# Attention scores in two column halves of TensorE, two query tiles in a row

## The chip, the core and the metric

The kernel runs on one core of one Trainium2 chip. The metric is device time in microseconds (us) from the start to the end of one execution, taken as the median of the runs. A core has five engines that run side by side, each through its own list of instructions in order: TensorE (PE) multiplies matrices, with PEld its loading of the stationary operand; VectorE (DVE) and ScalarE (ACT) work on rows of 128 partitions[...]; GpSimd (POOL)[...]; SyncE (SP) issues DMAs. They meet through semaphores.

## The reference

Two transformer layers with adaptive layer norm, in fp32, on x of 4 x 512 x 512. The first layer is small. The second holds nearly all of the time: attention with 32 query heads of 128 in 8 groups (four query heads share one key and one value head), causal, over 512 positions, for 4 batches; then a gated feed-forward layer of width 1792.

```python
q = (hidden_states @ w_q).reshape(B, S, Hkv, g, D)
k = (hidden_states @ w_k).reshape(B, S, Hkv, D)
v = (hidden_states @ w_v).reshape(B, S, Hkv, D)
scores = jnp.einsum('bqhgd,bkhd->bhgqk', q, k) * scale
causal = jnp.tril(jnp.ones((S, S), dtype=bool))
scores = jnp.where(causal, scores, -jnp.inf)
probs = jax.nn.softmax(scores.astype(jnp.float32), axis=-1).astype(q.dtype)
attn = jnp.einsum('bhgqk,bkhd->bqhgd', probs, v)
attn = attn.reshape(B, S, Hq * D)
return attn @ w_o
```

The change concerns the line of `scores`, the causal mask, and what follows them up to the softmax.

## The kernel before

The first 209 us compute the first layer and the first projections. From 209 to about 1709 us runs the attention of the second layer, and after it the feed-forward layer.

**Blocks, heads, tiles.** There are 32 blocks n (4 batches x 8 key heads), each with four query heads, so 128 heads s in all, and 64 pairs of heads. A head's 512 queries are four tiles i of 128. Because of the causal mask, tile i needs the keys up to (i + 1) x 128 only. `score(s, i)` (L872 to L887) makes one product on TensorE, 128 queries by (i + 1) x 128 keys, into a PSUM bank (L878); VectorE adds the mask to the last 128 columns (L879) and takes the negated maximum of each row (L881); ScalarE writes the exponentials to SBUF with their sums (L883). `divide` (L889) takes the reciprocal of the sum on VectorE and multiplies on ScalarE; `flip` (L895) transposes blocks of 32 x 32 on VectorE. When a pair is done, `carry` (L911) issues 16 DMAs that complete the transposition, and `value` (L920) multiplies the transposed probabilities with the values and copies the result from PSUM to `oT` on ScalarE (L933).

**Projections.** q, k, v and the output projection are done by Strassen's scheme with seven products. A product is a piece: `seven` (L738) writes it to a bank called `quarter` (L746), and VectorE adds it to what it belongs to (L778, L780, L842); the first of each seven is copied by ScalarE (L786).

**Order.** The order of work on each engine is that in which the program issues it. `window(w, ...)` (L1120) is the unit: it scores pair w + 1 and multiplies pair w with its values. Its eight score tiles go into slots 0 to 7: first head's tiles 3, 2, 1, 0, then the second head's. In slot i the program issues the transposition of the tile two slots back, the division of the tile one slot back, the score of this slot's tile, and then this slot's share of the projection pieces and of side work (statistics of a layer norm, or reads of weight blocks for their largest magnitude, L954). The two value products come in slots 8 and 9. Windows of two kinds alternate: one carries the pieces of q and part of k or v, the other the pieces of the output projection and the rest of k or v.

**Banks.** [...] Scores rotate through four: pools `ps_mm` and `ps_tr`, two banks each, taken in turn by the parity of i (L875), so that a tile's product waits for the exponentials of the tile four slots earlier. The pieces and half of the value products share three banks (`ps_sc`), and one bank is for the other value products.

Of the kernel before, what the change touches and what calls it, by code (L numbers as in the profile page):

```python
# [8 lines left out]
F32 = mybir.dt.float32  # L9
# [4 lines left out]
ALU = mybir.AluOpType  # L14
# [3 lines left out]
P = 128  # L18
# [6 lines left out]
HKV, G, D1 = 8, 4, 128  # L25
INTER = 1792
FB = 256
EPS = 1e-5
NEG = -3.0e38
EXACT = 4096.0  # L30


@with_exitstack
def adaln_two_layers(ctx: ExitStack, tc: tile.TileContext, a, out: bass.AP):
    nc = tc.nc
# [9 lines left out]
    conste = early.enter_context(tc.tile_pool(name="conste", bufs=1))  # L45
    lnp = early.enter_context(tc.tile_pool(name="ln", bufs=1))
    gap = early.enter_context(tc.tile_pool(name="gate_a", bufs=B))
    ps_mm = early.enter_context(tc.tile_pool(name="ps_mm", bufs=2, space=PSUM))
    ps_sc = early.enter_context(tc.tile_pool(name="ps_sc", bufs=3, space=PSUM))
    ps_tr = early.enter_context(tc.tile_pool(name="ps_tr", bufs=2, space=PSUM))  # L50
# [83 lines left out]
    with tc.using_default_side("right"):  # L134
# [15 lines left out]
    nc.vector.memset(mhalf, -0.5)  # L150
    ident = const.tile([P, P], F32, name="ident")
    make_identity(nc, ident)
    mask = conste.tile([P, P], F32, name="mask")
    nc.gpsimd.memset(mask, 0.0)
    nc.gpsimd.affine_select(
        out=mask, in_=mask, compare_op=ALU.is_ge, fill=NEG, base=0,
        pattern=[[-1, P]], channel_multiplier=1,
    )

    o_sb = [l0w.tile([P, NT, 32], F32, name=f"o{b}") for b in range(B)]  # L160
    for b in range(B):
# [3 lines left out]
        cid, pattern=[[0, 1]], base=0, channel_multiplier=1,  # L165
# [54 lines left out]
    ADD, SUB = ALU.add, ALU.subtract  # L220
# [5 lines left out]
    def left_sums(eng, t, s):  # L226

        A11, A21, A12, A22 = quarters(t)
        S3, S2, S4 = s[:, 0], s[:, 1], s[:, 2]
        eng.tensor_tensor(S3, A11, A21, SUB)  # L230
        eng.tensor_tensor(A21, A21, A22, ADD)
        eng.tensor_tensor(S2, A21, A11, SUB)
        eng.tensor_tensor(S4, A12, S2, SUB)
        return {1: A11, 2: A12, 3: S4, 4: A22, 5: A21, 6: S2, 7: S3}
# [15 lines left out]
    def sums_in(kind, n):  # L250
        w = weights[kind, n]
        s = T["wp"].tile([P, 3, 2, w.shape[2] // 2], F32, tag=f"s{kind}", name=f"s{kind}")
        left[kind, n] = left_sums(nc.gpsimd, w, s)
# [455 lines left out]
    for o in order:  # L709
        name, _, eng = o.partition("/")  # L710
# [24 lines left out]
    def bank(shape, name):  # L735
        return ps_sc.tile(shape, F32, tag="sc", name=name)
# [18 lines left out]
    qT, kT, vs, oT, prob = {}, {}, {}, {}, {}  # L755
# [8 lines left out]
    def sums_h(b, engs):  # L764
        s = hp.tile([P, 4, 2, HALF], F32, tag="hT", name="hsum")
        right["h", b] = right_sums(engs, h1[b], [s[:, i] for i in range(3)], s[:, 3])
# [40 lines left out]
    def q_pieces(n):  # L807
        def start():
            for j in range(2):
                qT[n, j] = at.tile([P, 2, S], F32, tag="qT", name="qT", bufs=3)  # L810
            return corners(qT[n, 0], qT[n, 1])

        return seven(lambda: left["q", n], lambda: right["h", n // HKV], gather(start), SEVENTH)
# [37 lines left out]
    BK = 32  # L851
    NG = P // BK
# [13 lines left out]
    def blocks(s, i):  # L866

        if s // 2 == LAST:
            return plain[:, s % 2, i, : (i + 1) * P].rearrange("p (j q) -> p j q", q=BK)
        return prob2[s // 2 % 2][:, : NG * (i + 1), s % 2, i, :]  # L870

    def score(s, i):  # L872
        n, h = divmod(s, G)
        w = (i + 1) * P
        pool, tag = ((ps_mm, "mm"), (ps_tr, "tr"))[i % 2]  # L875
        ps = pool.tile([P, 512], F32, tag=tag, name="sc")
        q = qT[n, h // 2][:, h % 2, :]
        nc.tensor.matmul(ps[:, :w], q[:, i * P : w], kT[n][:, :w], start=True, stop=True)  # L878
        nc.vector.tensor_tensor(ps[:, i * P : w], ps[:, i * P : w], mask, ADD)  # L879
        nmx = small.tile([P, 1], F32, tag="nmx", name="nmx")  # L880
        nc.vector.tensor_reduce(nmx, ps[:, :w], AX.X, ALU.max, negate=True)  # L881
        den = small.tile([P, 1], F32, tag="den", name="den")
        nc.scalar.activation(  # L883
            blocks(s, i), ps[:, :w].rearrange("p (j q) -> p j q", q=BK),
            AF.Exp, bias=nmx, accum_out=den,
        )
        prob[s, i] = den  # L887

    def divide(s, i):  # L889
        p = blocks(s, i)  # L890
        rden = small.tile([P, 1], F32, tag="rden", name="rden")
        nc.vector.reciprocal(rden, prob.pop((s, i)))  # L892
        nc.scalar.mul(p, p, rden)  # L893
# [17 lines left out]
    def carry(pair):  # L911

        for a_ in range(NG):
            src = prob2[pair % 2][a_ * BK : (a_ + 1) * BK]
            src = src.rearrange("r (k j) h i q -> r j k (h i q)", j=NG)
            for j in range(NG):
                dst = turned[j * BK : (j + 1) * BK, :, a_]
                nc.sync.dma_start(dst, src[:, j])

    def value(s):  # L920

        n, h = divmod(s, G)
        if h == 0:
            oT[n] = at.tile([P, G, S], F32, tag="oT", name="oT")
        av = bank([P, 512], "av") if s % 2 else ps_av.tile([P, 512], F32, tag="av", name="av")
        pT = straight if s // 2 == LAST else turned
        for k in range(NT):
            nc.tensor.matmul(  # L928
                av.rearrange("p (a n) -> p a n", a=NG)[:, :, BK * k :], vs[n][:, k, :],
                pT[:, k, :, P * (s % 2) + BK * k : P * (s % 2 + 1)],  # L930
                start=(k == 0), stop=(k == NT - 1),
            )
        nc.scalar.copy(  # L933
            oT[n][:, h, :].rearrange("p (i a q) -> p a i q", a=NG, q=BK),
            av.rearrange("p (a i q) -> p a i q", a=NG, q=BK),
        )


    def scan(i):
# [122 lines left out]
    def decide():  # L1062
        size = small.tile([P, 1], F32, tag="size", name="size", bufs=1)
        nc.vector.tensor_reduce(size, sizes, AX.X, ALU.max)
        nc.vector.tensor_scalar(size, size, EXACT, None, ALU.is_gt)
        return size
# [9 lines left out]
    def split_pieces(got):  # L1076

        def piece(c):
            if c == 0:
                h2[0] = [hp.tile([P, KC, S], F32R, tag="hT", name=f"h2_{i}") for i in range(2)]  # L1080
            pt, m = bank([P, S], "lnT"), modT[1]
            for t in range(NT):
                nc.tensor.transpose(
                    pt[:, t * P : (t + 1) * P], got["xn"][:, t, c * P : (c + 1) * P], ident
                )

            tag, bufs = (("v", 4), ("kT", 3))[c % 2]
            tm = at.tile([P, E], F32, tag=tag, name="tm", bufs=bufs)
            nc.scalar.activation(
                tm, pt, AF.Identity, bias=m[:, 2, c, 0:1], scale=m[:, 3, c, 0:1]  # L1090
            )
            hi, lo = (h[:, c, :] for h in h2[0])
            nc.scalar.copy(hi, tm)

            lows.append(lambda: nc.vector.tensor_tensor(lo, tm, hi.bitcast(F32), SUB))

        lows = []
        return [lambda c=c: piece(c) for c in range(KC)], [lambda c=c: lows[c]() for c in range(KC)]
# [17 lines left out]
    def run(*fill):  # L1116
        for f in fill:
            f()

    def window(w, fill, side=(), late=(), values=(8, 9)):  # L1120


        fill, side = list(fill), list(side)
        more = w + 1 <= LAST
        tiles = [(2 * w + 2 + h, i) for h in range(2) for i in (3, 2, 1, 0)]

        lag, turn_ = (5, turn) if w + 1 == LAST else (2, flip)
        slots = lag + 7
        share = [len(fill) // slots + (i < len(fill) % slots) for i in range(slots)]
        each = -(-len(side) // slots)  # L1130
        for i in range(slots + 1):
            if more and i >= lag:
                turn_(*tiles[i - lag])
            if more and 0 < i < 9:
                divide(*tiles[i - 1])
            if more and i < 8:
                score(*tiles[i])
            for h in range(2):
                if w >= 0 and values[h] == i:
                    value(2 * w + h)  # L1140
            if i < slots:
                for _ in range(share[i]):
                    fill.pop(0)()
                for _ in range(each):
                    if side:
                        side.pop(0)()
        run(*late)
        if w + 1 < LAST:
            carry(w + 1)
# [5 lines left out]
    run(*put(2, x[2]))  # L1155
    sums_h(0, (nc.gpsimd, nc.vector))
    nc.gpsimd.memset(prob2[0], 0.0)
    sums_in("k", 0)
    sums_in("v", 0)
    sums_wo(0)  # L1160
# [9 lines left out]
    run(*put(3, x[3]), *put(0, x[0]), *put(1, x[1]))  # L1170
    q = q_pieces(1)
    window(-1, v_pieces(0))
    load("v", 1)
    pending = []
    begun = []

    for n in range(NBLK):
        b, g = divmod(n, HKV)
        ahead, behind = n + 1 < NBLK, n > 0
        if n > 0:  # L1180
            q = q_pieces(n + 1) if ahead else []
# [3 lines left out]
        kind, m = "vk"[n % 2], n // 2 + n % 2  # L1185
# [40 lines left out]
        else:  # L1226
            first_weights()
            t, r = split_pieces(got)
# [5 lines left out]
            s = at.tile([P, 3, 2, HALF], F32, tag="soT", name="soT", bufs=1)  # L1234
# [262 lines left out]
```

## Time and profile before

| | |
|---|---|
| median of 3 runs | 2057.37 us (2057.35 to 2057.42) |
| profiled execution, its own time | 2058.11 us |
| its span, first to last instruction | 2056.2 us |
| TensorE busy over the span | 2020.9 us, 98% |
| VectorE busy | 1362.9 us, 66% |
| ScalarE busy | 878.9 us, 43% |
| GpSimd busy | 756.9 us, 37% |
| granted TensorE clock, mean | 0.987 |
| attention, 209 to 1709 us: TensorE busy | 1492.7 of 1500 us |
| L878, products of the scores | 1024 records, 355.1 us |
| L879, mask, VectorE | 512, 281 ns each in the median |

A fp32 product appears as two MATMUL records with a weight load each. The end of a matmul record is modelled: records of a stream overlap, so that the mean duration is longer than the step from one start to the next, and a busy share near 100% says that TensorE never waits, not that it works at its peak. A window lasts about 23 to 24 us. Where the chain of work names a line, that is where the time of the last finisher went.

### The profile page before, as it was taken

The page shows a single profiled execution, that of the slowest core. Times are in us where ns is not written, and L with a number is a line of the kernel's source. Part 1 is how long each engine was busy: PE and PEld are TensorE (multiplying, and loading weights), DVE is VectorE, ACT ScalarE, POOL GpSimd, SP SyncE. Part 2 cuts the span into 40 slices and gives each one's busy share as a digit, 9 for nine tenths or more (in the row PEclk, how much of TensorE's full clock was granted, in tenths as well). Part 3 has the DMA queues.
Part 4 walks back from the last instruction along what each step waited for, and adds up shares of the span by engine and source line. Part 5 has one row for each costly group of instructions (what it writes and reads, how often), then busy time and mean ns, then how long its engine had stood idle before and what let it go on. Part 6 is the DMA issues. An engine that isn't in the chain of part 4 may idle for free.

```text
span 2056.2 us, 27492 instructions
## 1 busy us (share of the span) xinstructions
PE 2020.9 (98%) x9219; PEld 1580.4 (77%) x9219; DVE 1362.9 (66%) x3323; ACT 878.9 (43%) x1998; POOL 756.9 (37%) x656
## 2 busy tenths in 40 slices
PE   6999999999999999999999999999999999999998
PEld 4655777878787887877787878787877777888887
DVE  6766776677667666766677676667666674655554
ACT  3421554445444444544444445444444454223322
POOL 2314234434336443353473334337333333800000
PEclk8799999999999999999999999999999999999999
DMA  8310656676657766655766665567656556600000
GB/s 299 123 62 30 173 151 175 159 175 153 144 144 192 180 160 161 164 144 152 186 182 163 154 164 133 144 154 177 167 144 154 141 128 202 196 21 1 21 21 22
DMA packets 243640, 288.59 MB, mean 140 GB/s; under 512 B 23250, under 2 KB 184018, under 8 KB 243492
## 3 DMA queue, kind: packets, MB, share of 16 engines
q1 hardware_dynamic: 242964, 285.71, 52.8%
q8 instruction: 76, 1.25, 0.3%
q10 hardware_dynamic: 528, 1.05, 0.2%
q14 instruction: 72, 0.59, 0.1%
HBM read 142.99 MB, written 11.57 MB: 75 GB/s over the span
## 4 chain that ended last, share of the span: by engine, by line
PE 94%; DVE 3%; ACT 1%; issue 1%; DMA 1%; POOL 0%; SPq 0%; DVEq 0%; ACTq 0%
PE quarter L746 46%; PE av L928 14%; PE sc L878 13%; PE p_gate L1347 5%; PE p_up L1347 5%; PE acc L1366 4%; PE ffn L634 2%; PE lnT L477 1%; PE modps L390 1%; PE lg L593 1%; PE qkv_ps L507 1%; PE modT_ps L403 1%; PE add_ps L578 1%; DVE bnst L60 0%; DMA c_sb<-in_L_cT_dram 0%
## 5 line engine op out<-in xcount | busy, mean ns | idle before, releaser
L878 PE MATMUL sc<-kT,qT 128*128 128x512 f32 (+3 forms) x1024 | 355.1, 433 | 0.0
L928 PE MATMUL av<-x,v 128*128 128x512 f32 x1008 | 295.7, 437 | 3.7 <-DMA x<-p 3.7
L928 PEld LDWEIGHTS av<-x,v 128*128 128x128 f32 x1008 | 190.3, 192 | 110.7 <-issue 66.5
L881 DVE TENSOR_REDUCE nmx<-sc 128x1 f32<-128x512 f32 (+3 forms) x512 | 251.6, 491 | 17.7
L893 ACT ACTIVATE x<-x,rden 128x512 f32<-128x512 f32 (+3 forms) x256 | 143.6, 561 | 235.4 <-DVE rden L892 235.4
L778 DVE TENSOR_TENSOR qT<-qT,quarter 128x512 f32<-128x512 f32 x224 | 150.5, 684 | 133.9 <-PE quarter L746 127.7
L893 ACT ACTIVATE p<-p,rden 128x512 f32<-128x512 f32 (+3 forms) x256 | 143.7, 561 | 221.5 <-DVE rden L892 219.8
L879 DVE TENSOR_TENSOR sc<-sc,mask 128x128 f32<-128x128 f32 x512 | 145.5, 284 | 136.5 <-PE sc L878 135.6
L842 DVE TENSOR_TENSOR acc<-acc,quarter 128x512 f32<-128x512 f32 x196 | 134.5, 686 | 134.6 <-PE quarter L746 134.4
L230 POOL TENSOR_TENSOR sq<-wq 128x512 f32<-128x512 f32 x32 | 40.6, 1269 | 471.5 <-DMA wq<-in_L_attn_w_q_dram 453.0
L878 PEld LDWEIGHTS sc<-kT,qT 128*128 128x128 f32 x1024 | 182.6, 191 | 24.2
L746 PEld LDWEIGHTS quarter<-wo,oT 128*128 128x128 f32 x744 | 140.9, 190 | 43.9 <-issue 20.1
L746 PE MATMUL quarter<-wo,oT 128*128 128x256 f32 x744 | 171.1, 379 | 0.2 <-ACT oT L933 0.2
L883 ACT ACTIVATE p<-sc,nmx 128x512 f32<-128x512 f32 (+3 forms) x256 | 135.1, 528 | 75.8 <-DVE nmx L881 67.1
L883 ACT ACTIVATE x<-sc,nmx 128x512 f32<-128x512 f32 (+3 forms) x256 | 134.9, 527 | 70.1 <-DVE nmx L881 65.4
L933 ACT COPY oT<-av 128x512 f32<-128x512 f32 x128 | 74.3, 581 | 167.0 <-PE av L928 165.0
L896 DVE STREAM_TRANSPOSE p<-p 128x512 f32<-128x512 f32 (+3 forms) x256 | 129.4, 506 | 2.0 <-ACT p L893 0.5
L896 DVE STREAM_TRANSPOSE x<-x 128x512 f32<-128x512 f32 x248 | 125.0, 504 | 1.3 <-ACT x L893 0.9
L746 PE MATMUL quarter<-hsum,sq 128*128 128x256 f32 x512 | 121.1, 379 | 1.4 <-DVE hsum L244 1.4
L746 PEld LDWEIGHTS quarter<-hT,wq 128*128 128x128 f32 x512 | 97.2, 190 | 32.4 <-issue 14.8
L746 PE MATMUL quarter<-hsum,wq 128*128 128x256 f32 x512 | 121.0, 379 | 0.0
L746 PE MATMUL quarter<-hT,wq 128*128 128x256 f32 x512 | 120.9, 379 | 0.0
(257 smaller groups left out, 3752.7 us busy)
## 6 DMA issues: line engine op xcount, KB each, us to landing
x<-p SPq DMA_DIRECT2D x512, 128.0 KB, 3.7
x<-x SPq DMA_DIRECT2D x496, 128.0 KB, 3.8
wq<-in_L_attn_w_q_dram SPq DMA_DIRECT2D x32, 1024.0 KB, 5.6
wo<-in_L_attn_w_o_dram SPq DMA_DIRECT2D x31, 1024.0 KB, 5.7
wm<-in_L_wmod_dram SPq DMA_DIRECT2D x12, 1024.0 KB, 9.6
wk<-in_L_attn_w_k_dram SPq DMA_DIRECT2D x16, 512.0 KB, 3.7
wv<-in_L_attn_w_v_dram SPq DMA_DIRECT2D x16, 512.0 KB, 3.8
xn<-x_d SPq DMA_DIRECT2D x28, 256.0 KB, 5.9
```

The costliest lines, as they stand in the source:

```text
L746: nc.tensor.matmul(ps[:, m, :], l[:, k, m * P : (m + 1) * P], r[:, k, :], start=(k == 0), stop=(k == 1),)
L778: nc.vector.tensor_tensor(c[out], c[v], ps, ADD if sign > 0 else SUB)
L842: nc.vector.tensor_tensor(osum[:, i - 1], osum[:, i - 1], ps, ADD)
L878: nc.tensor.matmul(ps[:, :w], q[:, i * P : w], kT[n][:, :w], start=True, stop=True)
L879: nc.vector.tensor_tensor(ps[:, i * P : w], ps[:, i * P : w], mask, ADD)
L881: nc.vector.tensor_reduce(nmx, ps[:, :w], AX.X, ALU.max, negate=True)
L883: nc.scalar.activation(blocks(s, i), ps[:, :w].rearrange("p (j q) -> p j q", q=BK), AF.Exp, bias=nmx, accum_out=den,)
L893: nc.scalar.mul(p, p, rden)
L896: nc.vector.transpose(blocks(s, i), blocks(s, i))
L928: nc.tensor.matmul(av.rearrange("p (a n) -> p a n", a=NG)[:, :, BK * k :], vs[n][:, k, :], pT[:, k, :, P * (s % 2) + BK * k : P * (s % 2 + ...
L1347: nc.tensor.matmul(ps[kind], w[kind][:, k, c * P : (c + 1) * P], h2[b % 2][i][:, k, :], start=(k == 0 and i == 0), stop=(k == KC - 1 and i ...
L1366: nc.tensor.matmul(acc[t], act[i][:, t * P : (t + 1) * P], w[:, c, :], start=(n == 0 and i == 0), stop=(n == NI - 1 and i == 1),)
```

## The change

The product of a score tile is cut into two halves of 64 queries. A half needs 64 keys fewer than its tile if it is the first half. TensorE's 128 columns are used as two tiles of 64 columns (`tile_position`): the same half of both heads of a pair is multiplied at one time, one in the lower and one in the upper 64 columns, and therefore partitions of PSUM. The second head's halves thus lie exchanged in their bank.

The four banks are now fixed tiles: one for each head of the pair and each parity of the query tile (`sc_ps`). `product` writes both heads of a query tile, and `score` calls it for two query tiles in a row: tiles 3 and 2 ahead of the first score of a window, tiles 1 and 0 ahead of the fifth. The slots follow: tiles 3, 3, 2, 2, 1, 1, 0, 0, the heads in turn. The mask is applied with the minimum of score and mask instead of their sum, so that what a first half leaves of older data in its last 64 columns is overwritten too; there are two masks, the second with its halves exchanged, and the four banks are filled with zeros once before the first product. For the second head of a pair the copy of the value product to `oT` becomes two copies that exchange the halves back.

```diff
--- before.py
+++ after.py
@@ -27,6 +27,7 @@
 FB = 256
 EPS = 1e-5
 NEG = -3.0e38
+TOP = 3.4028234e38
 EXACT = 4096.0
 
 
@@ -150,12 +151,15 @@
     nc.vector.memset(mhalf, -0.5)
     ident = const.tile([P, P], F32, name="ident")
     make_identity(nc, ident)
-    mask = conste.tile([P, P], F32, name="mask")
-    nc.gpsimd.memset(mask, 0.0)
-    nc.gpsimd.affine_select(
-        out=mask, in_=mask, compare_op=ALU.is_ge, fill=NEG, base=0,
-        pattern=[[-1, P]], channel_multiplier=1,
-    )
+    masks = conste.tile([P, 2, P], F32, name="masks")
+    nc.gpsimd.memset(masks, TOP)
+    HP = P // 2
+    for m, ps_, first_ in ((0, slice(0, P), 0), (1, slice(0, HP), HP), (1, slice(HP, P), 0)):
+        nc.gpsimd.affine_select(
+            out=masks[ps_, m], in_=masks[ps_, m], compare_op=ALU.is_ge, fill=NEG, base=first_,
+            pattern=[[-1, P]], channel_multiplier=1,
+        )
 
     o_sb = [l0w.tile([P, NT, 32], F32, name=f"o{b}") for b in range(B)]
     for b in range(B):
@@ -869,14 +873,31 @@
             return plain[:, s % 2, i, : (i + 1) * P].rearrange("p (j q) -> p j q", q=BK)
         return prob2[s // 2 % 2][:, : NG * (i + 1), s % 2, i, :]
 
+    sc_ps = [[p.tile([P, 512], F32, tag=t, name="sc") for _ in range(2)] for p, t in ((ps_mm, "mm"), (ps_tr, "tr"))]
+    def product(s, i):
+        n, h = divmod(s, G)
+        for half in range(2):
+            w = i * P + HP * (half + 1)
+            for h_ in range(2):
+                q = qT[n, (h + h_) // 2][:, (h + h_) % 2, :]
+                at_ = HP * (half ^ h_)
+                nc.tensor.matmul(
+                    sc_ps[h_][i % 2][at_ : at_ + HP, :w], q[:, w - HP : w], kT[n][:, :w],
+                    start=True, stop=True, tile_position=(0, at_),
+                )
     def score(s, i):
-        n, h = divmod(s, G)
-        w = (i + 1) * P
-        pool, tag = ((ps_mm, "mm"), (ps_tr, "tr"))[i % 2]
-        ps = pool.tile([P, 512], F32, tag=tag, name="sc")
-        q = qT[n, h // 2][:, h % 2, :]
-        nc.tensor.matmul(ps[:, :w], q[:, i * P : w], kT[n][:, :w], start=True, stop=True)
-        nc.vector.tensor_tensor(ps[:, i * P : w], ps[:, i * P : w], mask, ADD)
+        if s % 2 == 0 and i % 2:
+            product(s, i)
+            product(s, i - 1)
+        w, ps = (i + 1) * P, sc_ps[s % 2][i % 2]
+        nc.vector.tensor_tensor(ps[:, i * P : w], ps[:, i * P : w], masks[:, s % 2], ALU.min)
         nmx = small.tile([P, 1], F32, tag="nmx", name="nmx")
         nc.vector.tensor_reduce(nmx, ps[:, :w], AX.X, ALU.max, negate=True)
         den = small.tile([P, 1], F32, tag="den", name="den")
@@ -930,10 +951,13 @@
                 pT[:, k, :, P * (s % 2) + BK * k : P * (s % 2 + 1)],
                 start=(k == 0), stop=(k == NT - 1),
             )
-        nc.scalar.copy(
-            oT[n][:, h, :].rearrange("p (i a q) -> p a i q", a=NG, q=BK),
-            av.rearrange("p (a i q) -> p a i q", a=NG, q=BK),
-        )
+        dst = oT[n][:, h, :].rearrange("p (i a q) -> p a i q", a=NG, q=BK)
+        src = av.rearrange("p (a i q) -> p a i q", a=NG, q=BK)
+        if h % 2 == 0:
+            nc.scalar.copy(dst, src)
+        else:
+            nc.scalar.copy(dst[:, 2:], src[:, :2])
+            nc.scalar.copy(dst[:, :2], src[:, 2:])
 
 
     def scan(i):
@@ -1122,7 +1146,7 @@
 
         fill, side = list(fill), list(side)
         more = w + 1 <= LAST
-        tiles = [(2 * w + 2 + h, i) for h in range(2) for i in (3, 2, 1, 0)]
+        tiles = [(2 * w + 2 + h, i) for i in (3, 2, 1, 0) for h in range(2)]
 
         lag, turn_ = (5, turn) if w + 1 == LAST else (2, flip)
         slots = lag + 7
@@ -1155,6 +1179,8 @@
     run(*put(2, x[2]))
     sums_h(0, (nc.gpsimd, nc.vector))
     nc.gpsimd.memset(prob2[0], 0.0)
+    for ps in sc_ps[0] + sc_ps[1]:
+        nc.vector.memset(ps, 0.0)
     sums_in("k", 0)
     sums_in("v", 0)
     sums_wo(0)
```

## The prediction

> **What bounds the kernel now.** I read the page first, for the engine that carries the end. The first line below is part 1, the second part 4, the chain of work that ended last.
>
> ```profile
> PE 2020.9 (98%) x9219; PEld 1580.4 (77%) x9219; DVE 1362.9 (66%) x3323; ACT 878.9 (43%) x1998; POOL 756.9 (37%) x656
> PE 94%; DVE 3%; ACT 1%; issue 1%; DMA 1%; POOL 0%; SPq 0%; DVEq 0%; ACTq 0%
> ```
>
> TensorE is the bound. The view of busy time by stage says whether anything is left over in attention, 232 to 1690 us, and four short stages where the clock was lost (columns: stage, its length, busy time of PE, PEld, DVE, ACT, POOL, granted clock, DMA share, GB/s):
>
> ```profile
> 232.00:1690.00 1458.00, 1454.28 (x6663) 1158.03 (x6662) 1002.78 (x2702) 692.10 (x1689) 601.01 (x522) 1.00 0.63 158
> 233.70:237.10 3.40, 1.39 (x8) 1.06 (x6) 3.30 (x11) 1.92 (x6) 0.00 (x0) 1.00 0.89 204
> 237.10:243.90 6.80, 5.09 (x9) 2.95 (x10) 2.52 (x8) 2.75 (x8) 2.90 (x4) 0.50 0.36 104
> 1701.40:1704.90 3.50, 1.64 (x9) 1.05 (x9) 2.16 (x5) 3.47 (x10) 0.00 (x0) 0.99 0.90 268
> 1704.90:1711.70 6.80, 5.98 (x12) 3.98 (x13) 3.76 (x10) 4.51 (x13) 4.75 (x4) 0.50 0.56 193
> ```
>
> In 1458 us TensorE idles 3.7 us, all in one wait for a DMA. So attention takes what TensorE streams: a column saved is time saved, and any wait of TensorE is time lost. The other four rows: after 3.4 us with 1.9 to 2.0 us idle, the clock column reads 0.50 for 6.8 us, twice.
>
> The groups kept apart by form give the streaming rate. Score products of 128, 256, 384 and 512 columns last 274, 379, 487 and 593 ns: 0.83 ns per column plus a tail of 168 ns that overlaps the next instruction. Each fp32 product is two such records (1024 for 512 products).
>
> The timeline shows what a change of the array's tiling costs. L390 writes four column tiles of 32; L1070 has one output column:
>
> ```profile
> 85.92 0.66 PE L477 MATMUL lnT<-ident,xn 128*128 128x128 f32 x4
> 86.51 1.06 PE L390 MATMUL modps<-wm,silu_c 128*32 128x512 f32 x8
> 87.50 0.76 PE L507 MATMUL qkv_ps<-wcat,h1n 128*128 128x48 f32 x5
> ...
> 1291.98 0.19 PE L1070 MATMUL wide_ps<-ones,size 128*1 128x1 f32 x2
> 1292.10 0.91 PE L878 MATMUL sc<-kT,qT 128*128 128x384 f32 x2
> ```
>
> Eight records of 512 columns end in 1.06 us, twice 0.427 plus tail: four tiles run at once. But a successor normally starts 0.17 us before its predecessor's end, and here only 0.07 before, going in and coming out: 0.10 us of drain each way. The two records after L1070 take 0.91 us against 0.81 elsewhere: 0.10 us of a 128-column weight load that nothing hides.
>
> Last, one window (a pair of heads scored while an earlier pair is multiplied with the values), TensorE then VectorE, then ScalarE:
>
> ```profile
> 928.43 1.02 PE L878 MATMUL sc<-kT,qT 128*128 128x512 f32 x2
> ...
> 937.50 1.02 PE L878 MATMUL sc<-kT,qT 128*128 128x512 f32 x2
> ```
>
> ```profile
> 935.99 0.70 DVE L896 STREAM_TRANSPOSE x<-x 128x512 f32<-128x512 f32 x1
> ...
> 938.82 0.29 DVE L881 TENSOR_REDUCE nmx<-sc 128x1 f32<-128x128 f32 x1
> ```
>
> ```profile
> 939.15 0.37 ACT L883 ACTIVATE x<-sc,nmx 128x128 f32<-128x128 f32 x1
> ```
>
> TensorE starts the fifth score tile 9.07 us into the window. The exponential that frees the fourth tile's PSUM bank ends at 939.52, 11.09 us in. TensorE is 2.0 us ahead, and today this costs nothing: a tile reuses the bank of four tiles ago.
>
> [...]
>
> **The change, part by part.**
>
> *Streams.* Per pair, before: 2 heads x 2 records x (128+256+384+512) columns x 0.833 ns = 4.27 us. After, two 64-query halves run side by side, one of each head, equally wide: 2 records x (448+512+320+384 + 192+256+64+128 = 2304) x 0.833 = 3.84 us. Saved: 0.427 us, over 64 pairs 27.3 us. The total of weight columns is unchanged.
>
> *Modes.* A pair's products come in two rows (tiles 3 and 2, then 1 and 0), the full array between them: 128 excursions. Each: 0.10 in, about 0.05 for a first load of 64 columns (half the 0.10 seen), 0.10 out, 0.10 for the next 128-column load: 0.35 us, 45 us in all. Bounds: 0 if 64-wide tiles needn't drain; 0.53 if the alternation of tiles (low, high, high, low) also exposes three loads of 0.06. Net with the saving: +17.5 us (-27 to +41).
>
> *The bank wait.* The second row rewrites all four banks at once: tile 1's product needs the exponentials of tiles 3 of both heads, tile 0's those of tiles 2, the second of which is in slot 3, one slot earlier. I lay out the window above in the new order, t=0 at its start, same durations. TensorE: the first row ends at 3.12 (0.15 + 1.60 + 1.17 + 0.20), then the unchanged pieces of projection, 1.73 + 3.46 + 0.86 + 0.86, to 10.03; tile 1's products end at 10.92. There tile 0's want their bank. VectorE: the q piece of slot 1 leaves TensorE at 8.30, 1.6 us later than before; then, by the starts in the trace, its addition 8.50, transpose 9.10, reciprocal 9.73, mask 9.77, maximum (384 wide) 10.09, two additions for k 10.56 and 10.89, transpose (512 now, 384 before) 11.22, reciprocal 11.85, mask 11.89, maximum 12.21 to 12.77; ScalarE's exponential 12.81 and its accumulator read to 13.5. TensorE waits 13.5 - 10.9 = 2.6 us. Queued behind: all its work; nothing catches up, as TensorE has no idle time to give.
>
> The same lag, 2.0 us, stands in 24 windows of this kind (q and k pieces): 62 us. In four with layer-norm statistics it is 5.1 us; 5.5 each by the same layout, 22 us. Four short ones at the ends: 7 us. The other kind (output pieces) has TensorE later, 13.5; VectorE there ends at 13.7 (0.2 us, 8 windows) or, in 21 with two reads of a weight block of 0.6 us in slots 0 and 1, at 14.57 (1.05 us): 26 us with the first ones. Sum 117 us; the layout may be off 0.4 us a window, so 85 to 145.
>
> *The clock.* An idle of 1.5 us (at 190 us) left the clock at 1.00; 1.9 to 2.0 in one 3.4 us stretch halved it. [...] A halved spell of one stretch loses 1.7 us, of two 3.4; I take 2.2: 24 x 0.57 x 2.2 = 30, and 3 x 4 = 12 for the long waits. 42 us, bounds 0 and 85.
>
> *Edits at nothing or nearly.* ALU.min for ADD: same instruction, 281 ns. Two more mask fills and a larger fill on GpSimd (0.35 and 0.20 us each): under its 10.9 us of idleness before 13.45 us; without that cover about 1 us. Four PSUM fills on VectorE near 200 us: a 512-wide pass is 0.7 us, so 0 to 2.8; I take 1, as TensorE waits for VectorE in part there. The odd heads' copy in two: some 0.15 us more ScalarE per pair (two of about 0.37 for one of 0.58), ScalarE 46% busy in that window; if it delayed oT it would meet GpSimd's sums, not TensorE. The new order of tiles puts more into slots 0 to 3, counted above; the last transposes are of width 128 as before, so the DMAs of the transposed probabilities start no later relative to the window's end. VectorE's 135.6 us of waiting for score products mostly goes, which earns nothing.
>
> *Sum* against the profiled execution, 2058.1 us (span 2056.2 and 1.9 around it): + 17.5 + 117 + 1 + 42 = 2235.6; the median of the runs lies 0.7 below it: 2235.
>
> **Rivals.** (1) Waits as laid out but the clock holds: 2235 - 42 = 2193. For: 1.5 us idle did nothing. Against: the two halved spells. (2) The waits hardly bind, because VectorE no longer waits for products in slots 1 to 3: only modes remain, 2057 + 18 = 2075. Against: its chain hangs on the projection pieces, later by 1 to 2 us, which the layout contains. (3) The other side: mode changes hide. The place is the drain around each row; if it costs under 0.21 us, the streams saved (0.213 per row) win, up to 27 us: 2030. It decides only where VectorE and ScalarE free the fourth bank 2.6 us sooner than laid out. For: tiles start within ns of each other; against: 0.10 us each way, twice shown. (4) The change doesn't do what it says: the halves run one after the other, 246 us of stream more: over 2400. Against: L390.
>
> **How the numbers follow.** Forecast 50%, (1) 22%, (2) 13% (2060 to 2125), (3) 6%, (4) or a clock halved for longer 9%. The forecast's own range is 2195 to 2280; with (1) down to 2125 it leaves out most of (2), (3), (4). A measurement here tells 0.2% (4 us) from no change: faster 0.06, same 0.02, slower 0.92.
>
> **What would show it.** Score rows in 64-column form, 16 records in 2.8 and 1.1 us plus tails; drains of 0.10 us; a new wait "sc <- ACT" on TensorE of some 100 us in about 55 waits, longest 5 to 6 us; PEclk under 1 in attention. I am wrong if the wait is under 40 us, if rows take twice as long, or if the clock stays at 1.00.

## The result, and the profile after

The changed kernel takes 2220.03 us (2218.47 to 2221.7), against 2057.39 us: 1.079 times the time before, with a 95% interval of 1.0772 to 1.0809. The prediction was 2235 us, in a range of 2125 to 2280.

The page of the changed kernel, parts 1 and 4:

```profile
PE 2091.7 (94%) x10243; PEld 1559.4 (70%) x10243; DVE 1353.5 (61%) x3327; ACT 879.7 (40%) x2062; POOL 754.4 (34%) x658
PE 68%; DVE 12%; SPq 8%; DMA 6%; ACT 2%; issue 2%; POOL 1%; DVEq 0%; ACTq 0%
```

TensorE is no longer busy throughout: 94% instead of 98% of a longer span, and the chain of work that ended last, 94% TensorE before, now runs through VectorE and the DMA queue as well. The view of busy time by stage puts the idleness into attention (columns as before: length, PE, PEld, DVE, ACT, POOL, clock, DMA, GB/s):

```profile
232.00:1871.00 1639.00, 1541.95 (x7742) 1152.55 (x7741) 1002.22 (x2734) 706.51 (x1782) 608.85 (x532) 0.98 0.59 144
476.90:485.00 8.10, 2.40 (x18) 1.31 (x17) 6.63 (x21) 3.70 (x8) 1.02 (x1) 0.81 0.44 109
908.60:915.40 6.80, 5.10 (x16) 3.97 (x17) 2.88 (x10) 3.65 (x8) 0.00 (x0) 0.50 0.00 0
```

97 us idle where there were 3.7 before, and a clock under 1. The second row is one of the four windows with layer-norm statistics: in 8.1 us TensorE works for 2.4. The third is a stretch of half clock. The view of waits, for TensorE, names what it waits for:

```profile
PE sc L888 <- ACT x L904: 79.2, 61, 3.2
PE sc L888 <- ACT p L904: 14.8, 16, 1.7
PE quarter L750 <- DVE v L782: 1.5, 3, 0.5
```

L888 is the score product, L904 the exponential. Before, from 232 to 1690 us, the only wait was one of 3.7 us for a DMA. By form it is one product, that of tile 0's first half:

```profile
L888 PE MATMUL sc<-kT,qT 128*64 128x512 f32 x256 | 66.4, 592 | 0.0
...
L888 PE MATMUL sc<-kT,qT 128*64 128x64 f32 x256 | 39.8, 245 | 95.6 <-ACT x L904 79.2 <-ACT p L904 16.2
```

512 columns are streamed in 592 ns per record, as by the full array before (593), but two records at a time. The timeline of a window (TensorE; it starts at 1006.2 and is of the kind laid out in the prediction):

```profile
1006.27 3.02 PE L888 MATMUL sc<-kT,qT 128*64 128x448 f32 x16
1009.22 1.13 PE L750 MATMUL quarter<-hsum,wk 128*128 128x256 f32 x4
...
1016.32 0.98 PE L888 MATMUL sc<-kT,qT 128*64 128x192 f32 x8
1017.68 0.33 PE L888 MATMUL sc<-kT,qT 128*64 128x64 f32 x2 [0.38 <-ACT x L904]
1019.79 0.55 PE L888 MATMUL sc<-kT,qT 128*64 128x64 f32 x6 [1.79 <-ACT x L904]
1020.27 0.92 PE L750 MATMUL quarter<-hT,wq 128*128 128x256 f32 x3
```

Tile 1's products (192 columns and 256) are through by 1017.1; tile 0's wait first for tile 2 of the first head, then for that of the second. What they wait for, in VectorE's and ScalarE's timeline:

```profile
1017.50 0.70 DVE L917 STREAM_TRANSPOSE x<-x 128x512 f32<-128x512 f32 x1
1018.12 0.12 DVE L913 RECIPROCAL rden<-den 128x1 f32<-128x1 f32 x1
1018.16 0.28 DVE L900 TENSOR_TENSOR sc<-sc,masks 128x128 f32<-128x128 f32 x1
1018.48 0.56 DVE L902 TENSOR_REDUCE nmx<-sc 128x1 f32<-128x384 f32 x1
```

```profile
1019.07 0.58 ACT L904 ACTIVATE x<-sc,nmx 128x384 f32<-128x384 f32 x1 [0.18 <-DVE nmx L902]
1019.55 0.19 ACT L904 ACTIVATION_READ_ACCUMULATOR x<-sc,nmx 128x1 f32 x1
```

The exponential starts 12.9 us into the window (laid out: 12.81) and the bank is free at 13.6 (laid out: 13.5).

**Where 163 us went.** From the first score product to the first product of the feed-forward layer (`p_gate`) the trace has 1528.2 us before and 1692.0 after, +163.8: the whole difference. I sorted the time by the starts of the matmul records, whose ends are modelled. The stream of a row is its columns times 0.833 ns, two records at a time; the rate is the prediction's, 0.83 ns per column by the forms of 128 and 512 columns (274 and 593 ns). What it takes beyond that, from the end of the stream before it to the start of the next full-array record, is change of tiling and wait.

| | us |
|---|---|
| stream of the scores, 273.1 to 245.8 | -27 |
| change of tiling: 128 rows x (0.27 in the row + 0.107 in the first full-array record behind it) | +48 |
| second rows beyond their 0.27 us, and a few first ones: waits | +126 |
| records outside the rows while the clock is halved | +31 |
| everything else that was not stream: 35 before, 21 after | -14 |

The 126 us of wait are counted from the end of a stream; the 94 us of the view of waits begin only at the modelled end of the record before, 0.17 us later each time, and leave out the part that short waits hide in that tail. A part of the 126 in the long waits is work at half clock.

The last two lines belong together. Of the 35 us before, 11 were half clock too, in the kernel's own two spells, and about 3 the DMA wait that is nearly gone now. So half clock outside the rows grew by 20 us, from 11 to 31.

### The profile page after: what moved, and what is told of

Same layout as the page of the kernel before. It is cut to its first block, busy times and chain, and to the rows that moved or that the text cites. A ratio compares the mean times of both kernels' runs of the same rounds, so it can differ in the third digit from the quotient of the medians.

```text
span 2217.9 us, 29986 instructions
## 1 busy us (share of the span) xinstructions
PE 2091.7 (94%) x10243; PEld 1559.4 (70%) x10243; DVE 1353.5 (61%) x3327; ACT 879.7 (40%) x2062; POOL 754.4 (34%) x658
## 4 chain that ended last, share of the span: by engine, by line
PE 68%; DVE 12%; SPq 8%; DMA 6%; ACT 2%; issue 2%; POOL 1%; DVEq 0%; ACTq 0%
PE quarter L750 31%; PE av L949 12%; SPq L939 8%; PE sc L888 6%; PE p_gate L1373 4%; PE p_up L1373 4%; DMA x<-p 4%; PE acc L1392 4%; DVE nmx L902 2%; PE ffn L638 2%; DVE x L917 2%; DMA x<-x 2%; ACT x L904 1%; DVE sc L900 1%; DVE p L917 1%
## 5 line engine op out<-in xcount | busy, mean ns | idle before, releaser
L888 PE MATMUL sc<-kT,qT 128*64 128x448 f32 (+7 forms) x2048 | 306.9, 419 | 96.1 <-ACT x L904 79.2
L888 PEld LDWEIGHTS sc<-kT,qT 128*64 128x64 f32 x2048 | 134.8, 138 | 234.6 <-ACT x L904 96.8
L900 DVE TENSOR_TENSOR sc<-sc,masks 128x128 f32<-128x128 f32 x512 | 144.1, 281 | 180.3 <-PE sc L888 180.3
L904 ACT ACTIVATE p<-sc,nmx 128x512 f32<-128x512 f32 (+3 forms) x256 | 134.9, 527 | 110.8 <-DVE nmx L902 80.0
L750 PE MATMUL quarter<-wo,oT 128*128 128x256 f32 x744 | 177.1, 387 | 0.3 <-ACT oT L960 0.3
L904 ACT ACTIVATE x<-sc,nmx 128x512 f32<-128x512 f32 (+3 forms) x256 | 134.8, 526 | 101.7 <-DVE nmx L902 81.9
L750 PEld LDWEIGHTS quarter<-wo,oT 128*128 128x128 f32 x744 | 136.2, 190 | 39.3 <-issue 22.6
L750 PE MATMUL quarter<-hT,wq 128*128 128x256 f32 x512 | 144.4, 432 | 0.0
L750 PE MATMUL quarter<-hsum,wq 128*128 128x256 f32 x512 | 127.0, 393 | 0.0
L917 DVE STREAM_TRANSPOSE x<-x 128x512 f32<-128x512 f32 (+1 forms) x248 | 124.9, 504 | 1.2 <-ACT x L914 0.9
L750 PEld LDWEIGHTS quarter<-hT,wq 128*128 128x128 f32 x512 | 105.5, 214 | 22.3 <-issue 6.6
L750 PE MATMUL quarter<-so,soT 128*128 128x256 f32 x496 | 117.5, 380 | 1.5 <-DVE v L782 1.5
```

The costliest lines, as they stand in the source:

```text
L750: nc.tensor.matmul(ps[:, m, :], l[:, k, m * P : (m + 1) * P], r[:, k, :], start=(k == 0), stop=(k == 1),)
L888: nc.tensor.matmul(sc_ps[h_][i % 2][at_ : at_ + HP, :w], q[:, w - HP : w], kT[n][:, :w], start=True, stop=True, tile_position=(0, at_),)
L904: nc.scalar.activation(blocks(s, i), ps[:, :w].rearrange("p (j q) -> p j q", q=BK), AF.Exp, bias=nmx, accum_out=den,)
L917: nc.vector.transpose(blocks(s, i), blocks(s, i))
```

## The experiments

Each group of runs was compared with runs of the kernel before on the same chip: 2056.81 us in the median for the first four below, 2056.79 for the one with three rows and the first two with one row, 2056.0 for the one with two rows apart and the last.

**A row for each query tile.** Every row asks for a bank four slots after its last use.

```diff
-        if s % 2 == 0 and i % 2:
-            product(s, i)
-            product(s, i - 1)
+        if s % 2 == 0:
+            product(s, i)
```

> The change with one edit: a row holds one query tile of both heads, issued ahead of that tile's first score, so that a bank is asked for again four slots after its last use instead of one. Theory (the second row waits for exponentials one slot old: about 124 us, and half clock behind it 31 us; a change of tiling 0.27 us per row): waits of TensorE for ScalarE under 10 us, clock 1.00 in attention, 256 rows x 0.27 = 69 us against 27 us of stream saved: 2057 + 42 = 2099 us. Rival (the halves and changes of tiling are what is slow, the waits only follow from them): more changes, so 2220 us or more.

Measured: 2118.9 us, 1.0304 (1.0284 to 1.0325). TensorE's waits, and its attention stage:

```profile
PE sc L888 <- ACT x L903: 4.5, 4, 1.3
```

```profile
232.00:1771.00 1539.00, 1529.54 (x7735) 1105.89 (x7736) 1011.60 (x2732) 706.18 (x1786) 611.85 (x532) 1.00 0.62 153
```

The waits are all but gone, the clock is back at 1.00, and the time falls by 101 us although there are twice as many changes of tiling. The rival is out. The expected time was 20 us too low: I had left the 0.107 us of the exposed weight load behind each row out of the price, 27 us for 256 rows. The prediction's 0.35 us per row contains it. By the trace a row costs 0.26 + 0.107 = 0.37 us; the difference of the runs gives (2118.9 - 2056.8 + 27.3 - 4.5) / 256 = 0.33 us, because half clock and small waits outside the rows came to 13 us less than in the kernel before.

**The rows without the halves** (`full_array_rows`). Banks, rows and order of the change, products by the full array. The second head's mask and copy, which then need no exchange, are as the first's; these lines are left out here.

```diff
-        for half in range(2):
-            w = i * P + HP * (half + 1)
-            for h_ in range(2):
-                nc.tensor.matmul(
-                    sc_ps[h_][i % 2][at_ : at_ + HP, :w], q[:, w - HP : w], kT[n][:, :w],
-                    start=True, stop=True, tile_position=(0, at_),
-                )
+        w = (i + 1) * P
+        for h_ in range(2):
+            q = qT[n, (h + h_) // 2][:, (h + h_) % 2, :]
+            nc.tensor.matmul(
+                sc_ps[h_][i % 2][:, :w], q[:, i * P : w], kT[n][:, :w], start=True, stop=True
+            )
...
```

> Banks, rows of two tiles and order of the change, but the products by the full array, 128 queries at a time (no column tiles, no stream saved; the second head's mask and copy as the first's). Theory of the bank wait: the wait of some 120 us and the half clock of some 30 us stay, 2057 + 150 = 2207 us (2190 to 2215). Rival (tiling): nothing of the change's time is left, 2057 to 2065 us.

Measured: 2190.29 us, 1.0651 (1.063 to 1.0673). TensorE's waits:

```profile
PE sc L886 <- ACT x L901: 74.9, 61, 3.0
PE sc L886 <- ACT p L901: 13.6, 17, 1.6
```

133 us of the 163 come without any column tile, at the lower edge of the expected range, in 61 and 17 waits (61 and 16 with the halves), and half clock with them (54.6 us of attention halved, 75.1 with the halves). The wait belongs to the two tiles in a row. That the halves themselves add only 30 us to that also fits: 48 of tilings less 27 of stream, plus somewhat longer waits (94 us against 88.5) and more of the half clock.

**The order of the tiles alone** (`order_only`).

```diff
-        tiles = [(2 * w + 2 + h, i) for h in range(2) for i in (3, 2, 1, 0)]
+        tiles = [(2 * w + 2 + h, i) for i in (3, 2, 1, 0) for h in range(2)]
```

> The kernel before with the order of score tiles alone: 3, 3, 2, 2, 1, 1, 0, 0, heads in turn; products one at a time by the full array, banks in rotation. Theory of the bank wait: a bank is asked for four slots after its last use, so no wait: 2057 us within 4. Rival (the heavier first four slots hold up VectorE and with it TensorE, whatever the rows): 2100 us or more.

Measured: 2059.16 us over 21 runs, 1.0006 (0.9998 to 1.0015): no difference clear of the noise. The heavier first four slots are harmless while each product comes when its tile is due, with a bank four slots old.

**A change of tiling by itself**, added to the kernel before:

```diff
+        if s % 2 == 0 and i % 2:
+            nc.tensor.matmul(
+                ps[:64, :64], q[:, :64], kT[n][:, :64], start=True, stop=True, tile_position=(0, 0)
+            )
         nc.tensor.matmul(ps[:, :w], q[:, i * P : w], kT[n][:, :w], start=True, stop=True)
```

> The kernel before with 128 small products added, one ahead of tiles 3 and 1 of every pair's first head: 64 queries by 64 keys in the lower 64 columns, overwritten by the full product behind it. Each streams 2 x 64 columns, 0.11 us. If a change of tiling in and out costs 0.27 us as the rows show: 128 x 0.38 = +48 us, 2106 us. If it costs 0.35 us as predicted: 2116 us. If the change is hidden in a full stream: +14 us, 2071 us.

Measured: 2113.93 us, 1.028 (1.0259 to 1.0301): 57.1 us by 128, less 0.107 of stream, is 0.34 us. One of them in the timeline:

```profile
929.82 2.32 PE L932 MATMUL av<-x,v 128*128 128x512 f32 x8
932.07 0.33 PE L879 MATMUL sc<-kT,qT 128*64 128x64 f32 x2
932.33 1.13 PE L882 MATMUL sc<-kT,qT 128*128 128x512 f32 x2
```

932.07 is 0.07 us before the end of what came before, and so is 932.33: the 0.10 us of drain in the prediction, twice. The full product takes 1.13 us, 1.02 in the kernel before. I read this as its weight load: behind a row, the trace of the changed kernel starts that load together with the product (1009.21 and 1009.22 us), where the next load of the stream starts 0.21 us ahead of its product (1009.97 and 1010.18). The price of the prediction stands, 0.34 us measured for 0.35, and the stream of full-array records around it hid none of it.

**Three rows**: the second row split, tile 0 ahead of the seventh score.

```diff
-        if s % 2 == 0 and i % 2:
+        if s % 2 == 0 and i != 2:
             product(s, i)
-            product(s, i - 1)
+            if i == 3:
+                product(s, 2)
```

> The change with its second row split: tiles 3 and 2 in a row ahead of the first score, tile 1 ahead of the fifth, tile 0 ahead of the seventh. Theory: the wait goes as in the run with a row per tile, and 192 rows x 0.27 = 52 us stand against 27 us saved: 2057 + 25 = 2082 us. Rival (a row of two tiles ahead of the fifth is not the cause, the first row's lead is): TensorE still waits over 50 us, 2130 us or more.

Measured: 2107.89 us, 1.0246 (1.0225 to 1.0266). From 232 us on, TensorE waits for ScalarE in this product for 5.1 us, 5 times. So the row of tiles 3 and 2 at the window's start is innocent. The miss of 26 us is again the weight load (192 x 0.107 = 20) and some small waits of the pieces.

**Two rows, what they wait for older.** As many rows and banks as in the change:

```diff
+    sc_ps = [
+        {3: sc_b[0], 2: sc_b[2][:, :384], 1: sc_b[0][:, :256], 0: sc_b[3][:, 384:]},
+        {3: sc_b[1], 2: sc_b[3][:, :384], 1: sc_b[1][:, :256], 0: sc_b[2][:, 384:]},
+    ]
...
+        if s % 2 == 0 and i in (3, 1):
+            for k in (3, 2, 0) if i == 3 else (1,):
+                product(s, k)
...
-        tiles = [(2 * w + 2 + h, i) for i in (3, 2, 1, 0) for h in range(2)]
+        tiles = [(2 * w + 2 + h, i) for h, i in ((0, 3), (1, 3), (0, 2), (1, 2), (1, 0), (0, 0), (0, 1), (1, 1))]
```

> Two rows per pair and four banks as in the change, but what the second row waits for is older: the first row holds tiles 3, 2 and 0 of both heads (tile 0 of one head in the last 128 columns of the other's tile 2), the second holds tiles 1, in the banks of tiles 3, ahead of the seventh score, so six and five slots after those banks' last use. Theory: no wait and no half clock, 128 changes of tiling at 0.375 us (0.27 in the row, 0.107 for the weight load behind it) = 48 us against 27 us saved: 2057 + 21 = 2078 us. Rival (a second row in a window makes TensorE wait wherever it stands): 2150 us or more.

Measured: 2090.8 us, 1.0165 (1.0131 to 1.0199). TensorE's longest entries of waits from 232 us on:

```profile
PE quarter L750 <- DVE ve L1039: 7.3, 4, 1.9
PE pT L931 <- ACT tm L1117: 3.6, 2, 2.9
PE quarter L750 <- DVE v L782: 1.8, 4, 0.5
```

No score product is among them, nor in the rest of that view. Ahead of it, at the start of attention, one row waits for ScalarE once, 3.3 us up to 225.1 us, with 6.8 us of half clock around it. With 128 rows, as in the change, 129 us are gone. The 13 us above the expectation have three parts: about 13 us outside the rows, mostly pieces that wait for VectorE (11.5 us in the view of waits, 7.3 of them the first line), I take it to empty their banks; some 10 us in the rows, most of it that one row; and 10 us less half clock outside the rows than in the kernel before.

**One row per window.** All eight products in five banks; the even head's value product loses its bank to them. Then the same by the full array, and then with the even head's value product in a score bank that is free by that slot.

```diff
+    sc_ps = [
+        {3: sc_b[0], 2: sc_b[2][:, :384], 1: sc_b[4][:, :256], 0: sc_b[3][:, 384:]},
+        {3: sc_b[1], 2: sc_b[3][:, :384], 1: sc_b[4][:, 256:], 0: sc_b[2][:, 384:]},
+    ]
...
+        if s % 2 == 0 and i == 3:
+            for k in (3, 2, 1, 0):
+                product(s, k)
...
-        tiles = [(2 * w + 2 + h, i) for i in (3, 2, 1, 0) for h in range(2)]
+        tiles = [(2 * w + 2 + h, i) for h, i in ((0, 3), (1, 3), (0, 2), (0, 1), (1, 2), (1, 1), (0, 0), (1, 0))]
...
-        av = bank([P, 512], "av") if s % 2 else ps_av.tile([P, 512], F32, tag="av", name="av")
+        av = bank([P, 512], "av")
```

In the third run the last line reads:

```diff
+        av = bank([P, 512], "av") if s % 2 else sc_b[0]
```

> All four query tiles of a pair in one row at the window's start, in five banks: tiles 3 in one each, tile 2 of one head with tile 0 of the other, both tiles 1 in the fifth; the value products of both heads then share the three banks of the pieces; scores in the order 3, 3, 2, 1, 2, 1, 0, 0 so that neighbours lie in different banks. Theory: the row asks for its banks 2.5 us or more after their last use, so no wait, 64 rows x 0.27 = 17 us against 27 us saved: 2047 us, faster than before. Rival 1 (value products without a bank of their own hold up the pieces): 2060 to 2090 us. Rival 2 (a row of 32 records starves VectorE at the window's start and the lag returns at the next row): over 2090 us.

> The same one row in five banks, with products by the full array: neither stream saved nor tiling changed. Theory: 2057 us within 4, so that the difference to the run with one row of column halves, 10 us, is the balance of 27 us saved and 17 us of changes. Rival (bank layout itself costs): 2070 us or more.

> The one row in five banks, with the even head's value product in a score bank that is free by then (tile 3 of the first head), so that the pieces have their three banks with only the odd head's value product, as in the kernel before. Theory: the 33 us that the run of one row by the full array lost to waits for banks of the pieces go, and 64 x 0.375 = 24 us stand against 27 us saved: 2057 - 3 = 2054 us (2050 to 2058). Rival (the waits of the pieces come from the row's length at the start of the window, which puts VectorE behind): 2080 us or more.

Measured: 2085.46 us, 1.0134 (1.0117 to 1.0151); by the full array 2089.76 us, 1.0159 (1.0142 to 1.0176); with the bank given back 2084.16 us, 1.0134 (1.0114 to 1.0155). All three miss, by 38, 33 and 30 us. The halves gain 4.3 us over the full array, not the 10 expected of that pair; with the weight load behind each row in the price, 27 - 24 = 3 would have been the estimate. What is lost lies in the layout of one row. My reason for it, the value product without a bank of its own, fell with the third run: 1.3 us came back of 33. The longest waits of that run, from 232 us on, in attention:

```profile
PE quarter L750 <- DVE ve L1040: 7.3, 4, 1.9
PE sc L893 <- ACT oT L962: 5.8, 7, 1.4
PE quarter L750 <- DVE kT L784: 4.6, 5, 1.1
PE pT L932 <- ACT tm L1118: 3.3, 2, 2.7
PE quarter L750 <- DVE v L782: 2.6, 4, 1.1
PE quarter L750 <- DVE acc L846: 2.1, 6, 0.3
```

Four of the six lines, 16.6 us, are pieces waiting for VectorE. In the second the row waits for the copy out of the bank that I gave back; the fourth belongs to the transposes of the last pair. In the run by the full array the four lines of the pieces read 7.3, 4.6, 2.5 and 2.1. Before 232 us, in all three runs, one row waits once for ScalarE, 3.4 to 3.5 us. That the pieces, no longer spaced out by score products, follow each other faster than VectorE can add them up, as the rival had it, is a reading that fits; it was not tested by itself, and why one row loses 30 us stays open in part. No version that I ran is faster than the kernel before.

## Why the prediction was right

- **The bound.** TensorE had nothing to spare in attention, so each wait and each drain showed in full. Right: the whole difference lies there (+163.8 us).
- **Streams**, -27 us: right, two column tiles ran at once (592 ns for 512 columns, twice as many records, 245.8 us of stream).
- **Modes**, 45 us: right, 48 by the trace (0.377 us a row) and 0.33 to 0.34 us a row by two runs that count rows. The bound of 0.53, by loads exposed as tiles alternate, didn't come: the row itself takes 0.27 us over its stream.
- **The bank wait**, 117 us: right in mechanism, shown by taking it away three ways (2118.9, 2107.9 and 2090.8 us) and by keeping it alone (2190.3). By kind of window, measured beyond the 0.27 us: 2.65 to 2.8 us in the 24 windows laid out, 3.0 and 3.1 in two of them that ran into half clock (predicted 2.6); 6.6 to 6.8 in the four with statistics (5.5; part of it at half clock); 0 to 2 in the 21 with reads of weights, 17 us together (22); about 14 us at the two ends of attention (9). In all 126. The sign that I named was off in form: 77 waits, none longer than 3.2 us, for the two heads' products wait one after the other and each wait is listed alone.
- **The clock**, 42 us: right in kind, too high. Spells of half clock came behind all four long waits, but behind 10 of the 24 waits of 2.6 us, 42% of them; the factor of 0.57 in the prediction was my estimate, and no trace showed it. Nine of the ten lasted 3.4 us, the tenth 6.8. Measured outside the rows: 31 us, 20 more than the 11 that the kernel before had lost and that the base of 2058.1 contains. That is the term that was mis-sized.
- **The sum**, 2235 against 2220, is nearer than its terms: the clock is 22 us too high, waits 9 and modes 3 us too low, and the DMA wait of the kernel before, which the sum took as unchanged, lost some 3 us. That these errors cancel in part is luck.
- **Edits at nothing**: right. order_only is the kernel before within its noise, the score pass with the minimum still takes 281 ns, and attention began 1.7 us earlier than before, not later by the PSUM fills.
- **Rivals.** (1), the clock holds, is out: 16 spells of half clock. (2) fell with the 94 us of waits, (3) with the price of a row, (4) with the 245.8 us of stream.

## What to carry to other kernels

Where an engine is busy without a gap, ask of each reordering how old the last use of every buffer will be when it is asked for again: batching two tiles here turned a distance of four slots into one, and the wait cost more than four times what the halves could save. To find it ahead of time, lay one window's instructions out in the new order with the durations of the trace; for the wait in 24 of the windows it was right to 0.1 us. A column-tiled product inside a full-array stream paid 0.33 to 0.38 us here for going in and out, so it must save more than that at each visit.

## What was not expected of the hardware

- Waits that look alike differed in what came behind them. By the clock records of the changed kernel's trace, ten of the 16 spells of half clock in attention and at its end lasted 3.41 us and six 6.83 us. They came behind all four waits of 6.6 to 6.8 us, behind ten of the 24 of 2.65 to 3.1 us, behind one (2.11 us) of the four of 1.8 to 2.1 us, behind none of up to 1.3 us, and behind the last wait of attention (3.9 us). In the 3.41 us ahead of each spell TensorE was idle for 2.14 to 3.31 us, counted from the ends of the streams. Ahead of the two spells of the kernel before it was 2.2 us in this way (1.9 to 2.0 us in the view of stages). The length of the wait alone did not tell the ten from the other 14.
- The first full-array record behind a column-tiled row, of 256 columns, took 320 ns to the next start in the median, 216 ns in the stream: 0.107 us over the 213 ns of its own columns. Its weight load started with it (1009.21 and 1009.22 us, above). Loads within a row seem hidden: rows of 8, 16 and 32 records took 0.26, 0.27 and 0.29 us beyond their streams.
